# Routed expert blocks in pairs: gate and up of nine pairs by seven products, with the table of blocks made later

## The chip, the cores and the metric

The kernel runs on one core of one Trainium2 chip. The time is the device time of one execution in microseconds (us). The core has TensorE (PE; its weight loads are shown apart as PEld), VectorE (DVE), ScalarE (ACT), GpSimd (POOL) and SyncE (SP), which issues most of the DMAs. Everything is in float32. A float32 matrix product shows in the trace as two records, two *passes*, each with a weight load of its own; a transpose on PE is one pass.

## The reference

One layer of a transformer on 2 sequences of 1024 tokens with 512 channels: an attention-like part, and then a mixture of experts, which is where the change lies:

```python
h = _layernorm(x) * (1 + cb) + sb                      # 2048 tokens x 512
topk_w, topk_idx = jax.lax.top_k(softmax(h @ gate_w), 2)   # 2 of 8 experts
g = silu(einsum('td,edh->teh', h, w_gate)) * einsum('td,edh->teh', h, w_up)   # 352 hidden
routed = einsum('teh,ehd,te->td', g, w_down, comb)
shared = silu(h @ sw_gate) * (h @ sw_up) @ sw_down     # 704 hidden, all tokens
x = x + gb * (routed + shared)
```

Each token has two choices, so there are 4096 rows of routed work. They go to 8 experts in unequal numbers.

## The kernel before, in words

The 2048 tokens are 16 tiles of 128, or 4 groups of 512. After the attention part the kernel chooses two experts for each token and scatters the normalised token to a buffer in device memory, `hbuf`, where each expert has its own region of rows (`scatter`, L625, an indirect DMA issued by POOL). Behind the last row of each expert a block of zeros is scattered, from a tile `zeros_t` (L744), by eight more scatters. `block_table` (L742) works out on DVE how the rows fall into blocks of 128: a table `tbl` with the expert and the first row of each block, the number of blocks `nblk`, and for each choice the row at which its result will lie, `yrows`. There are at least 32 blocks (`NB0`), at most 39 (`NB`); in the profiled execution 35 ran.

While the scatters run, PE works on the shared expert of token group 1 (L1400 to L1406): five chunks of 128 hidden channels, each by `seven`, then the down projection `shared_down`. `seven` multiplies a 2 by 2 block matrix of gate and up weights with a 2 by 2 block matrix of tokens by seven products in place of eight, a Winograd form of Strassen's scheme: DVE makes four sums of weights (`mix_weights`, two chunks ahead) and four of tokens (`Tokens`), PE makes the products in PSUM, ACT copies the first one (L1024), and DVE adds them up in seven additions (L1026 to L1034) and gates the result with two multiplications (L1037, L1038). The products of a chunk take three of five PSUM banks named `mm` and one of three named `tr`, in turn; a bank is free again when DVE (or ACT) has read it. `shared_down` (L928) then multiplies the gated chunks with the down weights, chunk by chunk for two token tiles, and takes a chunk as soon as DVE has gated it. `keep_shared` (L1044, L1045) scales the result on DVE and adds it to the tokens on POOL.

Then come the routed blocks. SP reads the expert and the row of a block from the table, and asks for the rows (L1417) and the weights (L873 to L879) two blocks ahead, in three sets of weight tiles. A block is: transposes of the rows (L337) with a copy by ACT (L1450), gate and up products with the token rows as the stationary operand (L1458, 352 columns moving), sigmoid on ACT and two multiplications on DVE, three transposes of the result (L1470), copies by DVE, and three products with the down weights (L1486). The down products of a block stand behind gate and up of the next. The blocks past the 32nd stand in branches on the number of blocks.

Behind the blocks PE does the shared expert of token groups 2 and 3, for which DVE has made sums of weights and tokens beside the blocks (`made_behind`), while POOL gathers the routed results from `ybuf`.

Each engine works through its own instructions in one fixed order; an instruction that waits holds up all behind it on its engine. The order comes from a planner, which `tc.issue_after` can bind: the instructions in it come on their engine behind the one named. Tiles come from pools; `hrow` (L1157) held the normalised rows and `zeros_t` and is closed before `rpool` is opened (L1297) for the rows of the blocks, which takes room that other pools gave back. With `reuse_waits="tile"` the first write to a tile of such a pool waits for whatever last used the room that it lies in.

Of the kernel before, what the change touches and what calls it, by code (L numbers as in the profile page):

```python
# [18 lines left out]
P = 128  # L19
# [5 lines left out]
def kernel(  # L25
# [43 lines left out]

    NB = (TOPK * TOK + E * (P - 1)) // P  # L70

    NB0 = TOPK * TOK // P

# [18 lines left out]
    hlin = dram.tile([NT, P, D], FP, name="hlin")  # L92
    ybuf = dram.tile([NB * P, D], FP, name="ybuf")
    xres = dram.tile([4, P, D], FP, name="xres")
# [48 lines left out]
    blk_no = ramp([1, NB], [[1, NB]], "blk_no")  # L143
    blk_row = ramp([1, NB], [[P, NB]], "blk_row")
    upto = const.tile([P, E, E], FP, name="upto")
    nc.gpsimd.memset(upto, 0.0)
# [592 lines left out]

    tbl = const.tile([1, 2, NB], I32, name="tbl")  # L740
    nblk = const.tile([1, 1], I32, name="nblk")

    def block_table():
        zeros_t = hrow.tile([P, D], FP, tag="hr", name="zeros_t")  # L744
        nc.gpsimd.memset(zeros_t, 0.0)
        nc.sync.dma_start(hbuf[E * R : E * R + P, :], zeros_t)
        for i in range(NB0, NB):
            nc.sync.dma_start(ybuf[i * P : (i + 1) * P, :], zeros_t)
        ps = tr_ps("count")
        nc.tensor.matmul(ps[:, 0:E], ones_t, seen[:, NT, :], start=True, stop=True)  # L750
        cnt = table.tile([P, E], FP, name="cnt")
        nc.vector.tensor_copy(cnt, ps[:, 0:E])

        end = table.tile([P, E], FP, name="end")
        nc.vector.tensor_add(end, cnt, ex_end)
        endi = table.tile([P, E], I32, name="endi")
        nc.vector.tensor_copy(endi, end)
        for e in range(E):
            scatter(endi[:, e : e + 1], zeros_t)
        M = TOK // P  # L760
        more = table.tile([P, E, M], FP, name="more")
        nc.vector.tensor_tensor(
            more,
            cnt.unsqueeze(2).to_broadcast([P, E, M]),
            rows_b.unsqueeze(1).to_broadcast([P, E, M]),
            ALU.is_gt,
        )
        nball = table.tile([P, E], FP, name="nball")
        nc.vector.tensor_reduce(nball, more, AX.X, ALU.add)
        cu = table.tile([P, E, E], FP, name="cu")  # L770
        nc.vector.tensor_mul(cu, upto, nball.unsqueeze(1).to_broadcast([P, E, E]))
        cumall = table.tile([P, E], FP, name="cumall")
        nc.vector.tensor_reduce(cumall, cu, AX.X, ALU.add)
        nb, cum = nball[0:1, :], cumall[0:1, :]
        past = table.tile([1, NB, E], FP, name="past")
        nc.vector.tensor_tensor(
            past,
            blk_no.unsqueeze(2).to_broadcast([1, NB, E]),
            cum.unsqueeze(1).to_broadcast([1, NB, E]),
            ALU.is_ge,  # L780
        )
        be = table.tile([1, NB], FP, name="be")
        nc.vector.tensor_reduce(be, past, AX.X, ALU.add)
        nc.vector.tensor_mul(past, past, nb.unsqueeze(1).to_broadcast([1, NB, E]))
        st = table.tile([1, NB], FP, name="st")
        nc.vector.tensor_reduce(st, past, AX.X, ALU.add)
        nc.vector.scalar_tensor_tensor(st, st, -float(P), blk_row, ALU.mult, ALU.add)
        nc.vector.scalar_tensor_tensor(st, be, float(R), st, ALU.mult, ALU.add)
        nc.vector.tensor_scalar(st, st, float(E * R), None, ALU.min)
        nc.vector.tensor_scalar(be, be, float(E - 1), None, ALU.min)  # L790
        nc.vector.tensor_copy(tbl[:, 0, :], be)
        nc.vector.tensor_copy(tbl[:, 1, :], st)
        nc.vector.tensor_copy(nblk, cum[:, E - 1 : E])

        lead = table.tile([P, E], FP, name="lead")
        nc.vector.tensor_sub(lead, cumall, nball)
        nc.vector.scalar_tensor_tensor(lead, lead, float(P), ex_row, ALU.mult, ALU.subtract)
        pk = picks.rearrange("p t s e -> p (t s) e")
        nc.vector.tensor_mul(pk, pk, lead.unsqueeze(1).to_broadcast([P, NT * TOPK, E]))
        shift = table.tile([P, NT * TOPK], FP, name="shift")  # L800
        nc.vector.tensor_reduce(shift, pk, AX.X, ALU.add)
        rf = rowf.rearrange("p t s -> p (t s)")
        nc.vector.tensor_add(rf, rf, shift)
        nc.vector.tensor_copy(yrows.rearrange("p t s -> p (t s)"), rf)

# [196 lines left out]
    def seven(n, g, weights, b):  # L1002
# [35 lines left out]
        return on_act, nc.vector.tensor_mul(dst, dst, c2)  # L1038

    def keep_shared(t, ps):  # L1040

        z = xs[t // 4][:, t % 4, :]
        a = spare[:, t % 2, :]
        nc.vector.tensor_mul(a, ps, gb[t // NJ])  # L1044
        nc.gpsimd.tensor_add(z, z, a)  # L1045
# [236 lines left out]
    with tc.issue_after(placed[SPB].ins):  # L1282
# [4 lines left out]
    next(down)  # L1287
    ranks(NS - 1)
    table = hroom.enter_context(
        tc.tile_pool(name="table", bufs=1, side="right", reuse_waits="tile")  # L1290
    )
    block_table()
    hroom.close()
# [62 lines left out]
    def gather(t):  # L1356
        ys = []
        for s in range(TOPK):
            y = gpool.tile([P, D], FP, tag="sg", bufs=8, name=f"y{s}_{t}")
            nc.gpsimd.indirect_dma_start(  # L1360
                out=y,
                out_offset=None,
                in_=ybuf,
                in_offset=bass.IndirectOffsetOnAxis(ap=yrows[:, t, s : s + 1], axis=0),
                bounds_check=NB * P - 1,
                oob_is_err=True,
            )
            ys.append(y)
        return ys
# [25 lines left out]
    first = range(0, NS // 2)  # L1395
    last = range(NS // 2, NS)
    gTs[1] = gpool.tile([P, NF + 1, 512], FP, tag="gT", name="gT_1")
    half_up(1, up_part)
    toks[1].mix_3()
    for n in range(NF):  # L1400
        seven(n, 1, ready.pop(n), toks[1])
        if n + 2 < NF:
            ready[n + 2] = mix_weights(n + 2, up_part, s_stores[n % 2])
    for _ in shared_down(1, gTs[1], wds, keep_shared, tr_ps):
        pass


    def block_rows(i):
# [6 lines left out]
        )  # L1415
        hb = rpool.tile([P, D], FP, tag="hb", name=f"hb_{i}")
        nc.sync.dma_start(hb, hbuf[bass.ds(r, P), :])  # L1417
        return hb

    def block_weights(i, count=None):  # L1420
# [9 lines left out]
        def load():  # L1430
            load_weights(
                w,
                (
                    w_gate[bass.ds(e, 1)].rearrange("o d h -> (o d) h"),
                    w_up[bass.ds(e, 1)].rearrange("o d h -> (o d) h"),
                    w_down[bass.ds(e, 1)].rearrange("o h d -> (o h) d"),
                ),
            )

# [7 lines left out]
    def block_in(i, hb):  # L1447
        ps = transposes(hb, f"b{i}")
        hbT = rpool.tile([P, KC, P], FP, tag="hbT", name=f"hbT_{i}")
        nc.scalar.copy(hbT.rearrange("p k q -> p (k q)"), ps)  # L1450
        return hbT

    def block_hidden(i, hbT, w):
        pg = mm_ps(f"bg_{i}")
        pu = mm_ps(f"bu_{i}")
        for ps, wt in ((pg, w[0]), (pu, w[1])):
            for k in range(KC):
                nc.tensor.matmul(  # L1458
                    ps[:, :H], hbT[:, k, :], wt[:, k, :], start=(k == 0), stop=(k == KC - 1)
                )  # L1460
        gt = rpool.tile([P, H], FP, tag="gt", name=f"gt_{i}")
        gated(gt, P, pg, pu, f"b{i}", H)
# [4 lines left out]
    def block_turn(i, gt):  # L1467
        ps = tr_ps(f"gtr_{i}")
        for c, (h0, m) in enumerate(HCH):
            nc.tensor.transpose(ps[:m, c * P : (c + 1) * P], gt[:, h0 : h0 + m], ident)  # L1470
        gtT = rpool.tile([P, NH, P], FP, tag="gtT", name=f"gtT_{i}")
        if FULL:
# [10 lines left out]
    def block_out(i, gtT, w):  # L1483
# [7 lines left out]

        queue = nc.sync if i + 1 < NB0 else nc.scalar
        queue.dma_start(ybuf[i * P : (i + 1) * P, :], y)

# [12 lines left out]

    hbs = {i: block_rows(i) for i in range(2)}
    weights = {0: block_weights(0)}
    firsts = [shared_again_first(0), shared_again_first(1)]  # L1510
    weights[1] = block_weights(1)
    hbT = {0: block_in(0, hbs.pop(0))}
    turned = {}

# [10 lines left out]
    def block(i, ahead=NB):  # L1525
# [7 lines left out]
        if i + 1 < ahead:  # L1533
            hbT[i + 1] = block_in(i + 1, hbs.pop(i + 1))
        if i - 1 in turned:
            finish_block(i - 1)
# [26 lines left out]
    made_behind = {}  # L1563
    for i, g in enumerate(last):
        for j, name in enumerate(("mix_12", "mix_3", "mix_4")):
            made_behind[10 + 3 * i + j] = getattr(toks[g], name)
    for n in range(len(s_stores)):
        made_behind[17 + 2 * n] = lambda n=n: make_ready(n)

# [49 lines left out]
    )  # L1619
    for g in last:  # L1620
        gTs[g] = endp.tile([P, NF + 1, 512], FP, name=f"gT_{g}")
    s_last = endp.tile([P, 4, 2 * P], FP, name="s_last")
    for n in range(NF):
        for g in last:
            after = seven(n, g, ready[n], toks[g])
# [3 lines left out]
        if n == 1:  # L1629
            with tc.issue_after(after[1].ins):  # L1630
                ready[NF - 1] = mix_weights(NF - 1, up_part, quarters(s_last))
    for g in last:
        half_up(g, up_part)
        next_sum()
    spare = act_tile(4, "spare_again")
    for g in last:
        for _ in shared_down(g, gTs[g], wds, finish, tr_ps, apart=(g == NS - 1)):
# [70 lines left out]
```

## Time and profile before

| what | value |
|---|---|
| median of 3 runs | 769.61 us (768.76 to 770.23) |
| the profiled execution, its own time | 772.12 us |
| span of its instructions | 770.3 us |
| mean granted TensorE clock | 0.994 |
| PE busy | 751.9 us, 2527 passes |
| DVE busy | 428.7 us, 979 instructions |
| ACT busy | 232.5 us |
| POOL busy | 214.9 us |
| moved by DMA | 158.91 MB, 206 GB/s over the span |

By stage, times from the start of the span:

| stage | us | PE busy | DVE busy | DMA, GB/s |
|---|---|---|---|---|
| shared expert of group 1, five chunks and the half one, and the table | 312.0 to 347.8 | 35.12 | 32.36 | 198 |
| its down projection | 347.8 to 367.4 | 19.60 | 3.62 | 263 |
| 28 of the blocks, none of them at an edge | 375.05 to 600.14 | 225.09 | 57.20 | 339 |

A line of the timeline gives the start, the busy time of the merged instructions, the engine, the line of the kernel, the operation, the tile written and the tiles read, the shape, and how many there are; in brackets stands the idle time of the engine before it and what ended that. A busy time runs to the end of the last pass in the pipeline, so how fast passes follow each other is read from one start to the next.

### The profile page before, as it was taken

The numbers are of one execution on the slowest core, as the hardware profiler recorded it, in microseconds if no ns is written. First come the engines' busy times: TensorE is split into PE (matmuls) and PEld (weight loads), VectorE is DVE, ScalarE is ACT, GpSimd is POOL, SyncE is SP. The second block draws the span as 40 slices with busy tenths as digits, with TensorE's granted clock in tenths as the row PEclk, the third lists the DMA queues.
The fourth block names the chain that finished last, engine by engine and source line by source line (L and its number), as shares of the span: only waits on it lengthen the run. The fifth ranks groups of instructions, "written<-read, shape, count | busy, mean of one in ns | idle before, by whom it ended". The sixth has DMA issues, their size and how long they took to land. (4 is left out here: it accounts for less than half of the span.)

```text
span 770.3 us, 8477 instructions
## 1 busy us (share of the span) xinstructions
PE 751.9 (98%) x2527; PEld 415.8 (54%) x2527; DVE 428.7 (56%) x979; ACT 232.5 (30%) x495; POOL 214.9 (28%) x241
## 2 busy tenths in 40 slices
PE   7999999999999999999999999999999998999997
PEld 2444444444444444684565656656566554888542
DVE  3888956898736888982222123222221121499964
ACT  4664523557643153110122122221221212122310
POOL 1234524863632687562100000000000000234530
PEclk9999999999999999999999999999999999999999
DMA  8950001212335711367999999999999884624551
GB/s 322 383 170 16 14 0 69 109 57 67 137 96 195 269 68 42 123 260 252 337 352 347 348 344 334 343 339 325 330 338 331 292 287 161 193 83 136 166 163 55
DMA packets 96369, 158.91 MB, mean 206 GB/s; under 512 B 8089, under 2 KB 51097, under 8 KB 96321
## 3 DMA queue, kind: packets, MB, share of 16 engines
q1 hardware_dynamic: 89984, 138.41, 53.6%
q0 software_dynamic: 5760, 18.88, 7.4%
q10 hardware_dynamic: 576, 1.05, 0.4%
q8 instruction: 22, 0.36, 0.2%
q14 instruction: 27, 0.21, 0.1%
HBM read 128.15 MB, written 30.16 MB: 206 GB/s over the span
## 5 line engine op out<-in xcount | busy, mean ns | idle before, releaser
L1360 POOL DMA_INDIRECT y<-ybuf,yrows x32 | 37.0, 1156 | 336.0 <-SPq L1586 288.4
L410 PE MATMUL kv<-w_kv,xnT 128*128 128x512 f32 x256 | 115.2, 596 | 0.5 <-ACT xnT L393 0.5
L1486 PE MATMUL by<-wd_r,gtT 128*128 128x512 f32 (+1 forms) x210 | 96.1, 593 | 0.8 <-DVEq L1578 0.8
L1458 PE MATMUL bg<-wg_r,hbT 128*128 128x352 f32 x280 | 88.9, 460 | 0.9 <-ACT y L1490 0.9
L1458 PE MATMUL bu<-wu_r,hbT 128*128 128x352 f32 x280 | 88.5, 459 | 0.0
L410 PEld LDWEIGHTS kv<-w_kv,xnT 128*128 128x128 f32 x256 | 46.9, 190 | 57.2 <-issue 48.1
L1458 PEld LDWEIGHTS bu<-wu_r,hbT 128*128 128x128 f32 x280 | 53.2, 190 | 29.6
L1473 DVE COPY gtT<-gtr 128x256 f32<-128x256 f32 x35 | 14.9, 425 | 97.0 <-PE gtr L1470 97.0
L1458 PEld LDWEIGHTS bg<-wg_r,hbT 128*128 128x128 f32 x280 | 50.4, 190 | 23.5 <-ACT y L1490 1.3
L571 PE MATMUL o<-wp,xnT 128*128 128x512 f32 x128 | 57.3, 593 | 0.0
L1337 DVE TENSOR_TENSOR sg_b<-sg_b,bg 128x352 f32<-128x352 f32 x35 | 18.3, 521 | 68.8 <-ACT sg_b L1336 68.8
L1486 PEld LDWEIGHTS by<-wd_r,gtT 128*128 128x128 f32 (+1 forms) x210 | 37.2, 191 | 34.5 <-issue 33.5
L1450 ACT COPY hbT<-tr_b 128x512 f32<-128x512 f32 x36 | 21.1, 586 | 101.1 <-PE tr_b L337 101.1
L1338 DVE TENSOR_TENSOR gt<-sg_b,bu 128x352 f32<-128x352 f32 x35 | 18.3, 521 | 47.2 <-PE bu L1458 47.2
L1490 ACT COPY y<-by 128x512 f32<-128x512 f32 x35 | 20.5, 586 | 70.7 <-PE by L1486 48.9
L571 PEld LDWEIGHTS o<-wp,xnT 128*128 128x128 f32 x128 | 23.8, 190 | 28.6 <-issue 27.0
L1336 ACT ACTIVATE sg_b<-bg 128x352 f32<-128x352 f32 x35 | 16.2, 464 | 76.1 <-PE bg L1458 76.1
L440 POOL TENSOR_TENSOR cross<-kv 128x128 f32<-128x128 f32 x16 | 12.6, 790 | 75.4 <-DVE kv L417 45.2
L530 PE MATMUL wp<-aw,wqT 128*128 128x512 f32 x64 | 30.0, 625 | 0.7 <-DVE aw L511 0.7
L433 ACT ACTIVATE sq<-kv 128x512 f32<-128x512 f32 x32 | 20.2, 630 | 27.2 <-DVE kv L417 25.6
L610 POOL TENSOR_TENSOR hr<-hr,cb 128x512 f32<-128x512 f32 x16 | 22.3, 1393 | 21.3 <-issue 7.2
L393 ACT ACTIVATE xnT<-tr_a,colsb 128x128 f32<-128x128 f32 x64 | 24.4, 455 | 11.0 <-PE tr_a L337 10.9
(319 smaller groups left out, 1264.7 us busy)
## 6 DMA issues: line engine op xcount, KB each, us to landing
wg_r<-in_w_gate_dram SPq DMA_DIRECT2D x35, 704.0 KB
wu_r<-in_w_up_dram SPq DMA_DIRECT2D x35, 704.0 KB
wd_r<-in_w_down_dram SPq DMA_DIRECT2D x35, 512.0 KB
hb<-hbuf SPq DMA_DIRECT2D x36, 256.0 KB
ybuf<-y SPq DMA_DIRECT2D x31, 256.0 KB
wd_r<-in_w_down_dram SPq DMA_DIRECT2D x35, 192.0 KB
wmod<-in_wmod_dram SPq DMA_DIRECT2D x6, 1024.0 KB
x<-in_x_dram SPq DMA_DIRECT2D x3, 1024.0 KB
```

Of the source, the lines that this page charges most:

```text
L393: turned1[t] = nc.scalar.activation(xnT[g][:, f, j * P : (j + 1) * P], ps[:, f * P : (f + 1) * P], AF.Identity, bias=colsb[:, 1, f : f + 1 ...
L410: nc.tensor.matmul(ps, xnT[g][:, k, j * P : (j + 1) * P], w_kv[:, i, k, :], start=(k == 0), stop=(k == KC - 1),)
L433: nc.scalar.activation(sq, kv[:, i, :], AF.Square, accum_out=ss[:, i : i + 1])
L530: nc.tensor.matmul(ps, wqT[:, k, f * P : (f + 1) * P], aw[:, k, :], start=(k == 0), stop=(k == KC - 1),)
L571: nc.tensor.matmul(ps, xnT[g][:, k, j * P : (j + 1) * P], wp[:, k, :], start=(k == 0), stop=(k == KC - 1),)
L610: nc.gpsimd.tensor_mul(h, h, cb1[b])
L1337: nc.vector.tensor_mul(sg[:m, :n], sg[:m, :n], pg[:m, :n])
L1360: nc.gpsimd.indirect_dma_start(out=y, out_offset=None, in_=ybuf, in_offset=bass.IndirectOffsetOnAxis(ap=yrows[:, t, s : s + 1], axis=0), b ...
L1450: nc.scalar.copy(hbT.rearrange("p k q -> p (k q)"), ps)
L1458: nc.tensor.matmul(ps[:, :H], hbT[:, k, :], wt[:, k, :], start=(k == 0), stop=(k == KC - 1))
L1486: nc.tensor.matmul(ps, gtT[:m, c, :], w[2][:m, c, :], start=(c == 0), stop=(c == NH - 1))
L1490: nc.scalar.copy(y, ps)
```

## The change

1. The routed rows are taken in 9 pairs of blocks (`NPAIR`) first, and then in blocks of 128: `NB0` becomes 14 and `NB` 21, so of the 35 blocks of the profiled execution 18 become 9 pairs and 17 stay. A pair is two full blocks of one expert. In it gate and up are done by seven products with the weights as the stationary operand, in pieces of 128, 128 and 96 hidden channels, and 128 tokens moving. The hidden result then lies with channels on partitions, so that its transposes and their copies go. The down products of a pair stand behind the hidden part of the next pair.
2. The table is made in two parts. `block_table` keeps the zeros, the counts and the scatters of zeros. `expert_tables` (a second table `tbl2` for the pairs, the table for blocks, 42 DVE operations) stands behind the third chunk of `seven` in the shared expert of group 1, and `choice_rows` (13 operations) behind the fifth. Both were one function at the head of that stage. The tiles of `expert_tables` are cut out of one tile of `rpool`, the first of tag `hb`.
3. The weights of the first pair are asked for ahead of the rows.
4. Rows of a pair are two loads; the sums of weights of the next pair are made on DVE between the additions of a pair; the sums of tokens lie in a tile that held `spare`. What is made for groups 2 and 3 beside the blocks comes at blocks 1 to 13 and not 10 to 23.

Cut to its core:

```diff
+    NPAIR = -(-(TOPK * TOK - E * (2 * P - 1)) // (2 * P))
+    NB = (TOPK * TOK + E * (P - 1)) // P - 2 * NPAIR
+    NB0 = TOPK * TOK // P - 2 * NPAIR
...
     for n in range(NF):
-        seven(n, 1, ready.pop(n), toks[1])
+        _, after = seven(n, 1, ready.pop(n), toks[1])
         if n + 2 < NF:
             ready[n + 2] = mix_weights(n + 2, up_part, s_stores[n % 2])
+        if n == 2:
+            with tc.issue_after(after.ins):
+                expert_tables(counts, Carved(rpool.tile([P, 2, D], FP, tag="hb", name="tables")))
+    with tc.issue_after(after.ins):
+        choice_rows()
     for _ in shared_down(1, gTs[1], wds, keep_shared, tr_ps):
         pass
...
+    class Pair:
+        def __init__(self, hbT, store):
...
+            nc.vector.tensor_sub(self.t1, self.b12, self.b11)
+            nc.vector.tensor_sub(self.t2, self.b22, self.t1)
+            nc.vector.tensor_sub(self.t3, self.b22, self.b12)
+            nc.vector.tensor_sub(self.t4, self.b21, self.t2)
...
+    def pair_hidden(j, weights, b, steps):
+        a11, a12, a22, s1, s2, s3, s4 = weights
+        def product(name, a, h):
+            ps = mm_ps(f"{name}_{j}")
+            for c, (h0, m) in enumerate(HCH):
+                for k in range(KH):
+                    last[j] = nc.tensor.matmul(
+                        ps[:m, c * P : (c + 1) * P], a[:, k, h0 : h0 + m], h[:, k, :],
+                        start=(k == 0), stop=(k == KH - 1))
+            return ps
...
+        m1 = product("m1", a11, b.b11)
+        both(nc.scalar.copy, c11, m1)
+        m2 = product("m2", a12, b.b21)
+        m6 = product("m6", s2, b.t2)
+        both(add, c12, c11, m6)
+        then(both(add, c11, c11, m2))
+        m7 = product("m7", s3, b.t3)
+        then(both(add, c22, c12, m7))
+        m5 = product("m5", s1, b.t1)
+        then(both(add, c12, c12, m5))
+        m3 = product("m3", s4, b.b22)
+        then(both(add, c12, c12, m3))
+        m4 = product("m4", a22, b.t4)
+        both(add, c21, c22, m4)
+        both(add, c22, c22, m5)
...
-    hbs = {i: block_rows(i) for i in range(2)}
-    weights = {0: block_weights(0)}
+    ws = {0: pair_weights(0)}
+    hps = {j: pair_rows(j) for j in range(2)}
+    ws[1] = pair_weights(1)
     firsts = [shared_again_first(0), shared_again_first(1)]
-    weights[1] = block_weights(1)
-    hbT = {0: block_in(0, hbs.pop(0))}
...
+    token_rooms = act_tile(4, "token_sums").rearrange(...)
+    steps, sums = pair_sums(ws[0], sum_rooms[0])
+    with tc.issue_after(kept_shared[5].ins):
+        for step in steps:
+            step()
+    pair_of = {0: Pair(pair_in(0, hps.pop(0)), token_rooms[:, 0])}
...
+    for j in range(NPAIR):
...
+        gTp[j] = pair_hidden(j, sums, pair_of.pop(j), steps)
+        sums = next_sums
+        if j + 1 < NPAIR:
+            with tc.issue_after(last[j].ins):
+                turned_pair = pair_in(j + 1, hps.pop(j + 1))
+            pair_of[j + 1] = Pair(turned_pair, token_rooms[:, n])
...
+        if j > 0:
+            pair_out(j - 1, gTp.pop(j - 1), ws.pop(j - 1))
```

`both` is one operation on 128 partitions by 256 elements and one on 96 by 128, for the 352 hidden channels. `then` puts the next of four sums of weights, 704 elements wide, behind an addition.

## The prediction

> **What bounds the kernel now.** I read the page's busy shares first.
>
> ```profile
> PE 751.9 (98%) x2527; PEld 415.8 (54%) x2527; DVE 428.7 (56%) x979; ACT 232.5 (30%) x495; POOL 214.9 (28%) x241
> ```
>
> PE is busy throughout, so a stage costs what PE does in it, plus PE's waits. Next, the timeline of PE in one routed block:
>
> ```profile
> 438.52 2.53 PE L1458 MATMUL bg<-wg_r,hbT 128*128 128x352 f32 x8
> ...
> 440.89 2.53 PE L1458 MATMUL bu<-wu_r,hbT 128*128 128x352 f32 x8
> ...
> 443.25 0.60 PE L337 MATMUL tr_b<-ident,hb 128*128 128x128 f32 x4
> ...
> 443.69 2.74 PE L1486 MATMUL by<-wd_r,gtT 128*128 128x512 f32 x6
> ...
> 446.27 0.49 PE L1470 MATMUL gtr<-ident,gt 128*128 128x128 f32 x3
> ...
> 446.60 2.53 PE L1458 MATMUL bg<-wg_r,hbT 128*128 128x352 f32 x8
> ```
>
> From start to start: 446.60 - 438.52 = 8.08 us a block, 0.296 us a pass of 352 columns, 0.43 of 512, 0.11 a transpose of 128. No wait stands in it.
>
> The stage in which the new table is put is different. The timeline of PE and that of DVE there (chunks 3 and 4 of `seven`, counted from 0, then the down projection):
>
> ```profile
> 345.20 1.03 PE L1016 MATMUL m<-mixed 128*128 128x256 f32 x4
> ...
> 347.80 2.74 PE L928 MATMUL sd<-wd_s0a,gT 128*128 128x512 f32 x6
> ```
>
> ```profile
> 340.78 0.41 DVE L1026 TENSOR_TENSOR c<-c,m 128x256 f32<-128x256 f32 x1
> ...
> 344.37 0.69 DVE L1038 TENSOR_TENSOR gT<-gT,c 128x512 f32<-128x512 f32 x1
> 345.48 0.42 DVE L1026 TENSOR_TENSOR c<-c,m 128x256 f32<-128x256 f32 x1 [0.41 <-issue]
> ...
> 349.51 0.69 DVE L1038 TENSOR_TENSOR gT<-gT,c 128x512 f32<-128x512 f32 x1
> ```
>
> DVE works right behind PE: its last gate ends at 350.20, and the down projection needs it at about 351.2. Here DVE has one microsecond to spare. And the timelines of POOL and SP:
>
> ```profile
> 340.13 0.98 POOL L625 DMA_INDIRECT hbuf<-zeros_t,endi  x1 [4.21 <-DMA hbuf<-zeros_t]
> 341.42 0.98 POOL L625 DMA_INDIRECT hbuf<-zeros_t,endi  x1 [0.30 <-issue]
> ...
> 349.33 0.99 POOL L625 DMA_INDIRECT hbuf<-zeros_t,endi  x1 [0.30 <-issue]
> ```
>
> ```profile
> 352.33 1.24 SPq L1417 DMA_DIRECT2D hb<-hbuf  x2
> ```
>
> The eight scatters of zeros follow each other at 1.28 us; the last packets of their queue land at 351.72, and SP's first load of rows, which needs them, starts at 352.33.
>
> **The pairs (gain).** Before: 2 x 8.08 = 16.16 us for two blocks. After: seven products of three pieces and two halves of the channels are 42 products, 84 passes with 128 columns moving; 8 transposes of rows; 12 down passes. Six transposes of the result go. The trace has no plain pass of 128 columns. A line through 0.2155 us (256 columns: four passes of L1016 in 0.862), 0.296 and 0.43 gives 0.1085, which is also what a transpose of 128 takes. The other end is the weight load: the eight passes with one column moving in L474 follow at 0.1117, loads of 128 columns back to back (their busy time of 0.97 less the last one's 0.19, over 7). I take 0.110: 84 x 0.110 = 9.24, + 8 x 0.11 = 0.88, + 12 x 0.43 = 5.16, makes 15.28. Gain 0.88 a pair, **-7.9** for nine; with 0.1085, -9.1; with 0.1117, -6.6. DMA falls from 2.6 MB in 8.08 us (339 GB/s) to about 3.2 MB in 15.3, so it covers itself better than before.
>
> The Trainium skill ("TensorE: Matmul & The Clock Gate", "Wait — 56ns, not 53.3ns?") speaks against this: with one decode path the sequencer spends about 62 ns on each matmul. If a load cost as much, a pass would be 0.124 and the nine pairs would lose 2.7 us in place of gaining 7.9. L474's 0.1117 for load and pass together, in eight passes, says less than that, but eight passes might come out of a queue.
>
> DVE within a pair, by start to start: 0.34 for 256 elements, 0.20 for 128, and 0.81 for 704 (0.68 us at 512 and 0.415 at 256 give 0.88 long, of which some 0.07 overlap, as at 256). Behind product m6: seven additions in two parts 3.8, four weight sums 3.2, eight gating operations 2.2, three token sums to t2 1.1, waits some 0.6: 10.9 us until the next pair's m6 may start. PE needs for the same stretch 48 passes 5.28, transposes 0.88, down products 5.16, m1 and m2 2.64: 13.96. So DVE is hidden by 3 us. At pair 1 there are no down products yet: PE would be there after 8.8, so it waits **+2.1** (1 to 3).
>
> **The table's new place (loss).** `expert_tables` comes behind chunk 2, in a tile of `rpool`. In the order of the changed program as built, its first operation (`more`) stands ahead of all additions of chunk 3 on DVE, and it waits for the eight scatters and eight plain writes that read `zeros_t`, whose room it takes. The old table lay in a pool of its own and waited for none. So DVE, done with chunk 2 at 340.8, stands until 352.1, with the additions of chunks 3 and 4 queued behind, and PE behind them:
> - PE does chunk 3, two of three banks of chunk 4, and stops at 345.20 (the row above), since the third needs the bank that chunk 3's second addition frees. That comes at about 354.0, after eight table operations.
> - DVE then does 42 table operations. The old ones took 24 (with three others) in 4.13 us, 314.06 to 316.31 and 319.95 to 321.83, 0.172 each; small independent ones follow at 0.10. Between 4.2 and 7.2, I take 6.3, since the new ones are of 72 and 168 elements, not 312. Chunk 3 takes 4.3 (340.78 to 345.06), chunk 4 4.2 (4.72 less 0.5 of waiting for PE). 352.1 + 6.3 + 8.5 = 366.9.
> - PE has chunk 4 and the first ten down passes done by then, and needs chunk 4's gate at the eleventh. Without the wait that would be at 347.80 + 10 x 0.43 = 352.1; now 366.9 + 0.2. **+15.0** (12.4 with 4.2 and 8.0; 16.4 with 7.2 and 9.0).
>
> The first weights of a pair, though asked ahead of rows, come only when `tbl2` is there, at about 356 against 354.1; 2.1 MB at 340 GB/s are 6 us, and they are wanted at 373: no cost. `choice_rows`, 3 us, lies beside ten down passes. The table operations gone from the stage's head freed DVE where PE did not wait for them: nothing.
>
> **The clock.** After the branches PE idles 2.1 us, and then the windows say:
>
> ```profile
> 655.00:659.00 4.00, 3.24 (x8) 2.59 (x9) 0.00 (x0) 0.00 (x0) 0.00 (x0) 0.62 0.20 72
> ```
>
> The granted clock (0.62, the third number from the end) is a half for 3.4 us; passes of 256 columns come at 0.43, 1.7 us lost. The 9 us idle at 345 to 354 must do the same, but what follows it is ahead of DVE anyway. Before the eleventh down pass PE idles 2.8 us again: **+1.2** (0 to 1.8). By the skill's rule (same page, "The HAM clock gate") the half clock comes after an idle window of some 3.4 us. The row shows it after 2.1. By the rule this term would be nothing; the measurement decides.
>
> **The first pair.** Its token sums lie where `spare` was, so they wait for POOL's last addition of `keep_shared` (L1045, 368.31 + 2.50 = 370.8, when the down projection ended at 367.4). t2 is there at 372.1. PE, after transposes 0.88 and m1, m2 2.64, would be at 370.9. **+1.2** (0.3 to 2).
>
> **Sum.** -7.9 + 2.1 + 15.0 + 1.2 + 1.2 = +11.6. On the profiled execution, 772.1, that is 783.7; it stands 2.5 over the median of 769.6, so a median of **781.2**. The ends together: -9.1 + 1 + 12.4 + 0 + 0.3 = +4.6, and -6.6 + 3 + 16.4 + 1.8 + 2 = +16.6: 774.2 to 786.2.
>
> **Rivals.**
> 1. *DVE isn't held by the scatters; the change is faster or even.* For it: the table's values don't depend on them, only its room does, and PE's gain in the pairs is plain arithmetic. Against: POOL's rows, which nothing in the change moves. Price: from 340.8, or up to 1.8 sooner since the old table is gone from the head, 6.3 + 8.5 give 353.8 to 355.6, a delay of 1.9 to 3.7; with -7.9, +2.1 and +1.2 and no half clock, -2.7 to -0.9: 766.9 to 768.7, likeliest **767.8**. The point: the delay may be 4.6 for no change, so the first table operation would have to start by 340.8 + 4.6 - 3.7 = 341.7, when only the second of eight scatters is issued. Chance 0.10.
> 2. *A sustained stream of short passes is slower than eight of them show.* At the only long stream's spacing, 0.2155 (256 columns, which need it), a pair would take 24.1; that is the far end, +80 us over my sum. The nearer: 0.12 a pass, +0.84 a pair, +7.6: **789**. PE's loads would then stand apart. Chance 0.05.
> 3. *DVE sets the pairs.* If each of its 34 operations between m6 and t2 ran its full length with nothing overlapped (0.415, 0.28, 0.88), that is about 3 us more, 13.9: just PE's 13.96. With waits on top a pair may lose 1 us, +8: **789**. For it: DVE and PE would both be near full. Against: 3 us of slack as rows go. Chance 0.05.
>
> **Numbers.** Forecast 0.80, rivals 0.10, 0.05, 0.05. Range 774.2 to 786.2, leaving out the rivals. A measurement of this kernel can tell about 0.2%, 1.5 us, from no change. Of rival 1, 0.06 is faster by more than that and 0.04 within; all the rest, 0.90, is slower.
>
> **What would show it.** In the profile after: DVE idle from about 340 to 352 ahead of the first table operation, ended by a DMA of `hbuf`; PE idle from about 345 to 354 ahead of L1016's products, and again ahead of the down projection; its last pass at about 382 against 366.85; passes of the pairs at 0.11 from start to start, pairs at 15.3; about 2 us of waiting in pair 1, none in pairs 2 to 8. It is wrong if the table's first operation starts before 345, or if passes of 128 columns come slower than 0.12.

## The result: 779.89 us against 769.39, and the profile after

The changed kernel takes 779.89 us (four runs, 778.24 to 780.95), the kernel before beside it 769.39 (768.76 to 770.23). The ratio is 1.0126, with a 95% interval from 1.0107 to 1.0146: slower by 9.7 us (8.2 to 11.2). Forecast were 781.2 and a range from 774.2 to 786.2.

First the busy shares again, from the page of the changed kernel:

```profile
PE 745.3 (96%) x2941; PEld 440.8 (57%) x2941; DVE 497.0 (64%) x1211; ACT 239.6 (31%) x531; POOL 217.6 (28%) x243
```

PE does 6.6 us less than before (751.9), and the span is 6.2 longer: PE gained work time and lost more by waiting. The timeline of DVE shows where the wait begins:

```profile
336.12 0.69 DVE L1136 TENSOR_TENSOR gT<-gT,c 128x512 f32<-128x512 f32 x1
351.55 0.29 DVE L792 TENSOR_TENSOR tables<-cnt,rows_b 128x128 f32<-128x128 f32 x1 [14.74 <-DMA hbuf<-zeros_t,endi]
...
352.93 0.41 DVE L1125 TENSOR_TENSOR c<-c,m 128x256 f32<-128x256 f32 x1
...
363.43 0.69 DVE L1136 TENSOR_TENSOR gT<-gT,c 128x512 f32<-128x512 f32 x1
```

DVE has gated chunk 2 at 336.8 and then stands for 14.74 us, until the scatters of zeros have landed; by the trace's packet records their last packets do so at 350.44. L1125 is chunk 3's second addition. The last gate of chunk 4, at 350.20 before, comes at 364.1. The timeline of PE answers:

```profile
342.45 1.03 PE L1114 MATMUL m<-hT,wu_s0a 128*128 128x256 f32 x4
353.49 2.04 PE L1114 MATMUL m<-mixed 128*128 128x256 f32 x4 [10.02 <-DVE tables L850]
...
358.74 2.87 PE L1026 MATMUL sd<-wd_s0a,gT 128*128 128x512 f32 x6
...
364.17 1.13 PE L1026 MATMUL sd<-wd_s1a,gT 128*128 128x512 f32 x2 [0.85 <-DVE gT L1136]
...
379.56 0.66 PE L344 MATMUL tr_p<-ident,hp 128*128 128x128 f32 x4
```

PE stands 10.02 us behind DVE (the profile names the table operation that ended last; the addition L1125, which frees the bank, ends at 353.34). Then it works at half clock (from 355.33 to 357.03 it starts four passes of 256 columns, 1.70 us and not 0.86), and waits once more at the eleventh down pass.

Stages are compared from the first pass of the half chunk, `ph` (L1345 before, 314.32; L1446 after, 312.43), which lies ahead of everything that the change touches:

| stretch | before | after | difference |
|---|---|---|---|
| `ph` to the first down pass | 33.48 | 46.31 | +12.83 |
| `ph` to the first transpose of routed rows | 53.05 | 67.13 | +14.08 |
| from there to the first product of groups 2 and 3 | 288.39 | 283.74 | -4.65 |
| from there to the end of the span | 114.55 | 113.24 | -1.3 |

So the stage of the tables loses 14.1 us and the routed part wins 4.7 back (4.84, counted to the last down product of the blocks). The last row, and most of the 1.9 us ahead of `ph`, are a matter of the clock and not of the change: the profiled execution of before has half clock for 3.4 us at 99.6 and at 655.9, and that of the changed kernel at neither place.

A pair in the steady state:

```profile
408.94 2.82 PE L1599 MATMUL m<-hpT,wg_p 128*128 128x128 f32 x24
411.60 4.15 PE L1599 MATMUL m<-token_sums,sums 128*128 128x128 f32 x36
...
419.12 5.32 PE L1655 MATMUL py<-wd_p,pgT 128*128 128x512 f32 x12
424.28 2.82 PE L1599 MATMUL m<-hpT,wg_p 128*128 128x128 f32 x24
```

424.28 - 408.94 = 15.34 us, against 16.16 for two blocks. 36 passes in 415.59 - 411.60 = 3.99 are 0.1108 each.

### The profile page after: what moved, and what is told of

The parts are those of the page before. It is cut to its first block, busy times and chain, and to the rows that moved or that the text cites. A ratio compares the mean times of both kernels' runs of the same rounds, so it can differ in the third digit from the quotient of the medians.

```text
span 776.5 us, 9447 instructions
## 1 busy us (share of the span) xinstructions
PE 745.3 (96%) x2941; PEld 440.8 (57%) x2941; DVE 497.0 (64%) x1211; ACT 239.6 (31%) x531; POOL 217.6 (28%) x243
## 3 DMA queue, kind: packets, MB, share of 16 engines
q10 hardware_dynamic: 576, 1.05, 0.4%
## 5 line engine op out<-in xcount | busy, mean ns | idle before, releaser
L1611 DVE TENSOR_TENSOR pc<-pc,m 128x256 f32<-128x256 f32 x63 | 25.9, 412 | 36.7 <-PE m L1599 36.6
L1655 PE MATMUL py<-wd_p,pgT 128*128 128x512 f32 (+1 forms) x108 | 47.9, 592 | 0.0
L1745 PE MATMUL by<-wd_r,gtT 128*128 128x512 f32 (+1 forms) x102 | 46.7, 593 | 1.0 <-DVEq L1877 1.0
L1714 PE MATMUL bg<-wg_r,hbT 128*128 128x352 f32 x136 | 43.2, 460 | 0.9 <-ACT y L1749 0.9
L1714 PE MATMUL bu<-wu_r,hbT 128*128 128x352 f32 x136 | 43.0, 459 | 0.0
L1599 PE MATMUL m<-token_sums,sums 128*128 128x128 f32 x324 | 37.5, 275 | 1.4 <-DVE token_sums L1566 1.4
L1599 PEld LDWEIGHTS m<-token_sums,sums 128*128 128x128 f32 x324 | 36.4, 182 | 1.8 <-issue 1.2
L1714 PEld LDWEIGHTS bu<-wu_r,hbT 128*128 128x128 f32 x136 | 25.8, 190 | 14.4
L447 POOL TENSOR_TENSOR cross<-kv 128x128 f32<-128x128 f32 x16 | 12.6, 789 | 75.3 <-DVE kv L424 43.7
L1655 PEld LDWEIGHTS py<-wd_p,pgT 128*128 128x128 f32 (+1 forms) x108 | 19.8, 190 | 21.6 <-issue 19.9
L1714 PEld LDWEIGHTS bg<-wg_r,hbT 128*128 128x128 f32 x136 | 24.6, 190 | 12.6 <-ACT y L1749 1.3
L1646 ACT ACTIVATE pgT<-pc 128x256 f32<-128x256 f32 (+1 forms) x36 | 11.1, 356 | 60.1 <-DVE pc L1611 60.1
```

The costliest lines, as they stand in the source:

```text
L1599: last[j] = nc.tensor.matmul(ps[:m, c * P : (c + 1) * P], a[:, k, h0 : h0 + m], h[:, k, :], start=(k == 0), stop=(k == KH - 1),)
L1611: op(*(t[:, 0:full] for t in tiles))
L1655: nc.tensor.matmul(ps, gT[:m, c, i * P : (i + 1) * P], w[2][:m, c, :], start=(c == 0), stop=(c == NH - 1),)
L1714: nc.tensor.matmul(ps[:, :H], hbT[:, k, :], wt[:, k, :], start=(k == 0), stop=(k == KC - 1))
L1745: nc.tensor.matmul(ps, gtT[:m, c, :], w[2][:m, c, :], start=(c == 0), stop=(c == NH - 1))
```

## Experiments

Ratios are to the kernel before, run on the same chip, with 95% intervals.

| kernel | median, us | ratio |
|---|---|---|
| changed | 779.89 | 1.0126 (1.0107 to 1.0146) |
| before_wait | 781.3 | 1.0144 (1.0118 to 1.0171) |
| own_room | 769.17 | 1.0007 (0.9990 to 1.0023) |
| own_room_again | 766.86 | 0.9958 (0.9942 to 0.9975) |
| late_table | 772.15 | 1.0028 (1.0011 to 1.0045) |
| late_loads_behind | 767.85 | 0.9963 (0.9948 to 0.9979) |
| own_late | 766.58 | 0.9959 (0.9945 to 0.9973) |
| five_pairs | 768.88 | 0.9985 (0.9972 to 0.9998) |
| m3_early | 765.71 | 0.9945 (0.9923 to 0.9967) |
| m3_and_room | 765.27 | 0.9939 (0.9917 to 0.9961) |
| sums_ahead | 762.84 | 0.9900 (0.9884 to 0.9917) |
| wait_pe_busy | 780.06 | 1.0124 (1.0107 to 1.0141) |
| changed_pe_busy | 779.34 | 1.0121 (1.0102 to 1.0140) |

### The wait alone, in the kernel before (before_wait)

```diff
+        if n == 2:
+            with tc.issue_after(after.ins):
+                nc.vector.memset(rpool.tile([P, 3 * D], FP, tag="waits", bufs=1, name="waits")[:, 0:1], 0.0)
```

> The kernel before, with one operation more on DVE: behind chunk 2 it clears one column of a tile that lies in the room of zeros_t, so it waits for the eight scatters of zeros. No table is moved, no pair is made. My theory (DVE held by the scatters): DVE stands from 340.8 to about 352, then does chunks 3 and 4 in 7.5 to 8.5; PE stops at 345.2, goes on at half clock, and the eleventh down pass comes 8 to 9.5 late: 777.4 to 779. Rival (it is the work of the table, not the wait, that makes the change slow): the wait costs at most the one microsecond that DVE has too little, 769.4 to 771.

It takes 781.3, 11.1 us more than before by the ratio (9.1 to 13.2); that is 2.3 above the range that I expected. One operation of 0.06 us costs about as much as the whole change. DVE and PE in its timelines:

```profile
352.45 0.06 DVE L1406 MEMSET waits<- 128x1 f32 x1 [11.70 <-DMA hbuf<-zeros_t,endi]
```

```profile
344.35 1.03 PE L1016 MATMUL m<-hT,wu_s0a 128*128 128x256 f32 x4
353.54 2.05 PE L1016 MATMUL m<-mixed 128*128 128x256 f32 x4 [8.17 <-DVE c L1027]
```

PE stands 8.17 us, goes on at half clock until about 359, and the eleventh down pass and the first transpose of rows both come 11.2 us later than before, counted from `ph`. I had expected 8 to 9.5: PE at half clock is later at the down projection than DVE's last gate, of which more below. The rival, that the table's work and not the wait is what costs, is out.

### The tables in a room that nobody holds (own_room, own_room_again)

```diff
-                expert_tables(counts, Carved(rpool.tile([P, 2, D], FP, tag="hb", name="tables")))
+                expert_tables(counts, Carved(gtp.tile([P, NF + 1, 512], FP, tag="gT", name="tables")[:, 0:2, :]))
```

> The changed kernel, with the tiles of the tables cut from a tile that lay idle since the down projection of group 0; the instructions of every engine stand in the same order. My theory: the first table operation starts right behind chunk 2, at about 337, DVE does the 42 operations and chunks 3 and 4 in the 12.6 us that it took behind the wait, 349.4, in time for the eleventh down pass; what is left of the change is what the routed part gains, 4.65 as measured: 764.8 (763 to 767; my rival 1 had 766.9 to 768.7, with more for the operations of the table). Rival (the table's work costs, not the wait): 776 to 780. Rival (pairs lose, the table costs little): over 771.

769.17: some 9 us of the loss are gone by this one line, but 4.4 more were left than I expected. Its profile shows why. DVE doesn't wait for the scatters any more, yet PE waits for DVE at the down projection:

```profile
352.99 1.13 PE L1026 MATMUL sd<-wd_s1a,gT 128*128 128x512 f32 x2 [2.32 <-DVE gT L1136]
```

The table began at 339.98 and not at 337, because chunk 2's additions had begun 3.3 us later, counted from `ph`, than in the changed kernel (331.49), where the instructions of all engines stand in the same order. So I ran it again for its profile.

> The changed kernel with the tables in the idle room, once more, for its profile. There chunk 2's additions began 3.3 us behind the products that they read (334.7), and the eleventh down pass waited 2.3 for DVE. In the profile of the changed kernel, with the same order of instructions, they began at once (331.5). Theory A (the late start of chunk 2 is an accident of the execution, and it is what costs the 2.3): with a start at 331.5 the wait at the down projection is gone and the execution takes 765 to 766; with a start at 334 to 335 it is 2 to 2.5 again, 768 to 769. Theory B (the 42 operations alone cost it): 2.3 of waiting and 768.5 to 769.5, wherever chunk 2 starts.

The first addition of chunk 2, in own_room and then in own_room_again:

```profile
334.74 0.42 DVE L1124 TENSOR_TENSOR c<-c,m 128x256 f32<-128x256 f32 x1 [3.96 <-PE m L1114]
```

```profile
331.63 0.42 DVE L1124 TENSOR_TENSOR c<-c,m 128x256 f32<-128x256 f32 x1 [0.72 <-PE m L1114]
```

Here there is no wait at the down projection, and the first transposes come 53.05 us behind `ph`, exactly as before the change; in own_room they came 55.96 behind it. The median is 766.86. This speaks against B, with one profile on each side: the 42 operations behind chunk 2 cost nothing when chunk 2 is on time, and 2.9 us of the stage in the profile where it is late. That the lateness is an accident of the single execution, the other half of A, is not shown: all ten executions of own_room took 768.5 us or more, and all four of own_room_again, on another chip, 767.1 or less, though the kernels are the same. So it seems to hold for a whole batch of executions. Why is open (see the end).

### The tables later, in the held room and in the free one (late_table, own_late, late_loads_behind)

```diff
-        if n == 2:
+        if n == NF - 1:
```

> The changed kernel, the tables still in the room of zeros_t, but behind the fifth chunk in place of the third. The wait is there as before, but no addition or gate is queued behind it. My theory: DVE stands from about 348 to 351.5, does the tables until 357 and the rest by 360, beside the down projection; the weights of the first pair are asked for at 355 and wanted at 367: 764.8 to 767. Rival (a wait of DVE for the scatters costs wherever it stands, by way of the weights or of the down projection's banks): 770 to 776.

> Both: the tables in the idle room and behind the fifth chunk. My theory: like the one with the room alone, 764.8 (763 to 767), with DVE's work beside the down projection; if the 42 operations behind chunk 2 make the additions late, this one is faster by as much (up to 3). Rival (the place costs by the weights that come later): slower than the one with the room alone by 1 or more.

own_late takes 766.58 and is faster than the kernel before, by 3.2 us (2.1 to 4.2). In the free room the place makes no difference beyond the late chunk 2: in own_late's profile chunk 2 begins 3.2 us late too, and the first transposes still come 53.05 behind `ph`. late_table takes 772.15, and its rival is right: the wait costs here too. Its profiled execution took 769.12 (the ten run from 768.82 to 773.99); in it the first transposes come 57.97 behind `ph`, 4.9 late. DVE, SP's queue and PE:

```profile
355.63 0.29 DVE L792 TENSOR_TENSOR tables<-cnt,rows_b 128x128 f32<-128x128 f32 x1 [7.05 <-DMA s_again<-in_sw_gate_dram]
```

```profile
345.50 0.38 SPq L1412 DMA_DIRECT2D s_again<-in_sw_up_dram  x1
```

```profile
363.73 4.23 PE L1026 MATMUL sd<-wd_s0a,gT 128*128 128x512 f32 x6 [3.27 <-DVE spare L1144]
```

DVE stands until 355.6 and not 351.5. The profile names the load that landed last; the scatters' last packets landed at 354.57, and DVE starts 1.06 behind them, as it did 1.11 behind them in the changed kernel. While the first weights still waited for the table, two loads of 1 MB for the shared expert (`s_again`) came ahead of them on SP, at 345.5, in the midst of the scatters. The scaling L1144, which frees the banks of the down projection, stood behind the tables on DVE, and PE waited 3.27 for it. To tell the loads from the place, I bound them behind the rows of the pairs (`asked` holds the loads of these rows):

```diff
+    with tc.issue_after(asked[-1].ins):
         firsts = [shared_again_first(0), shared_again_first(1)]
```

> The kernel with the tables in the room of zeros_t behind the fifth chunk (772.2), but the two loads of 1 MB for the shared expert of groups 2 and 3 bound behind the rows of the first pairs, as they stood in the changed kernel. My theory (those loads, asked for at 345.5, held up the scatters of zeros from 351.5 to 354.6, and so DVE to 355.6): the scatters land at 351 again, DVE is done with the tables before PE needs the next bank at 360.4, and the time is that of the tables in the idle room, 766.6 (765.5 to 768). Rival (a wait of DVE behind the fifth chunk costs by way of the banks in any case): 770 to 773.

```profile
353.41 0.29 DVE L792 TENSOR_TENSOR tables<-cnt,rows_b 128x128 f32<-128x128 f32 x1 [3.90 <-DMA hbuf<-zeros_t,endi]
```

767.85, within the expectation. Counted from `ph`, the last packets of the scatters land 38.7 us behind it and not 41.9, DVE starts the tables 3.1 us sooner, and PE's wait of 3.27 is gone. The first transposes come 53.43 behind `ph`, so that of the wait 0.4 us is left.

### What a pair is worth (five_pairs)

```diff
-    NPAIR = -(-(TOPK * TOK - E * (2 * P - 1)) // (2 * P))
+    NPAIR = 5
```

> The kernel with the tables in the idle room behind the fifth chunk, but five pairs in place of nine (25 blocks in place of 17). My theory: each of four pairs gives up the 0.82 that the trace shows between 15.34 and two blocks at 8.08, +3.3: 769.9. Rival (the whole kernel gains little from pairs, since blocks and pairs wait for the same transfers): 766 to 767.5.

From the first transpose to the last down product of the blocks it takes 284.22 us, own_late 280.98: 3.24 for four pairs, 0.81 each, as the trace of one pair says. The median is only 2.0 to 2.3 above own_late's, between the theory and its rival, so the profiles carry this; own_late's profiled execution has a half clock window behind the branches (24 passes in 6.93 us, not 5.28), that of five_pairs has none. The rest is below what these runs can tell.

### Pair 1 (m3_early, m3_and_room, sums_ahead)

In the changed kernel, as in own_late, PE waits in pair 1:

```profile
396.18 4.22 PE L1599 MATMUL m<-token_sums,sums 128*128 128x128 f32 x36 [1.05 <-DVE token_sums L1566]
```

```diff
         m2 = product("m2", a12, b.b21)
+        m3 = product("m3", s4, b.b22)
         m6 = product("m6", s2, b.t2)
...
-        m3 = product("m3", s4, b.b22)
```

> The kernel with the tables in the idle room behind the fifth chunk (766.6), and in each pair the product m3 (sum of weights s4 by raw tokens) moved ahead of m6, so that PE has 1.33 us of work more before it needs the first sum of tokens. My theory (pair 1 waits 1.03 and the first pair 0.37 for the sums of tokens, because no down products lie between): both waits go, 1.4 less, 765.2; pairs 2 to 8 stay at 15.34. Rival (DVE or a bank of PSUM is the bound behind it, since m3 now holds its bank longer): 766.6 or more.

765.71, and half of the theory fell: the first pair's wait of 0.37 went (the routed part is 0.62 shorter), but pair 1's stayed at 1.05. DVE's chain runs from m6 of one pair to t2 of the next, and PE's products from m6 to m6 are the same ones in whatever order. Moving m3 from behind m6 to ahead of it moves both ends. The first pair's sums of tokens still waited on DVE for POOL, 2.0 us in the changed kernel as in this one; but PE no longer waited for them:

```profile
383.03 0.43 DVE L1565 TENSOR_TENSOR token_sums<-hpT 128x256 f32<-128x256 f32 x1 [2.01 <-POOL x L1145]
```

The next kernel also takes away that wait (the line is the changed kernel's). Its core:

```diff
-    token_rooms = act_tile(4, "token_sums").rearrange("p c q -> p (c q)").rearrange(
+    token_rooms = spare.rearrange("p c q -> p (c q)").rearrange(
...
-    pair_of = {0: Pair(pair_in(0, hps.pop(0)), token_rooms[:, 0])}
+    pair_of = {0: Pair(pair_in(0, hps.pop(0)), token_rooms[:, 1])}
```

> The same, and the sums of tokens of the first pair in the half of spare that POOL's last additions don't read, in place of a new tile over all of spare. My theory: DVE makes them at once behind its last scaling, 2 us sooner, but with m3 ahead PE no longer waits for them: 0 to 0.3 less than with m3 alone, 765.0. Rival (the first pair's 1.2 of my prediction was right, and hangs on POOL): 764.0.

765.27; the routed part is unchanged (280.37 us against 280.36), as expected. Last, work is taken out of the chain itself. `made` is the last sum of tokens of a pair:

```diff
+        if j == 0:
+            with tc.issue_after(pair_of[0].made.ins):
+                for step in steps:
+                    step()
+            steps = []
```

> The kernel with m3 ahead and the sums of tokens in spare (765.3), and the four sums of weights of pair 1 made before the additions of pair 0 and not between them, so that DVE has 3.2 us less between m6 of pair 0 and t2 of pair 1. My theory (that stretch of DVE sets pair 1): its wait of 1.05 goes, 1.0 to 1.3 less: 764.1. Rival (the weights of pair 1, asked for at 359, land too late, or pair 0's additions wait behind the sums): 765.3 to 766.5.

762.84, more of a gain than expected. The routed part is 0.98 shorter, and in pair 1 PE no longer waits for DVE:

```profile
382.13 4.15 PE L1599 MATMUL m<-spare,sums 128*128 128x128 f32 x36
```

Its wait for ACT at the head of pair 1 has grown from 0.24 to 0.56. The 0.98 is what I expected; the rest of the 2.4 to 3.0 us between the medians is in no stage of the profile, whose execution took 764.62 (the six run from 762.24 to 764.68). This is the fastest version: 1.0% faster than the kernel before (0.83 to 1.16%), 2.2% faster than the changed one.

### The half clock (wait_pe_busy, changed_pe_busy)

```diff
+        if n == NF - 1 and g == 1:
+            idle = tr_ps("idle")
+            for _ in range(10):
+                nc.tensor.matmul(idle, ident, hT[1][:, 0, :], start=True, stop=True)
         m5, m3 = products(mm_ps(f"m53_{n}_{g}"), (s1, b.t1), (s4, b.b22))
```

> The kernel before with the wait alone (781.3), and ten products of no use on PE (20 passes of 512 columns, 8.6 us) between the second and the third bank of chunk 4, where PE stood from 345.4 to 353.5. My theory: the granted clock stays whole, PE does the last products of chunk 4 and the first ten down passes 2.6 us sooner, and then waits for DVE's last gate (361.3) at the eleventh, which came at 363.3: 1.9 less, 779.4. Rival (the half clock has another cause, or costs nothing because DVE is as late): 781.3.

> The changed kernel (779.9) with the same ten products in the same place. My theory: the clock stays whole here too, but the eleventh down pass waits for DVE's last gate (364.1) in any case, which the tables hold up: no change, 779.2 to 780.6, and PE's wait at L1026 grows from 0.85 to some 3.4. Rival (the half clock is part of the delay, on top of the wait): 777.3.

In both the granted clock stays whole through the stage's wait. wait_pe_busy is 1.2 us below before_wait in the median and 1.1 in the profile, counted from `ph` to the first transposes. There the ninth down pass, the first of this kernel's order that reads chunk 4, comes at 361.24 and not at 362.5 (the third of the four passes from 361.61), and now waits for DVE (I had reckoned with the eleventh, and so with 1.9). First before_wait, then wait_pe_busy:

```profile
361.61 1.88 PE L928 MATMUL sd<-wd_s1a,gT 128*128 128x512 f32 x4
```

```profile
361.24 1.12 PE L928 MATMUL sd<-wd_s1a,gT 128*128 128x512 f32 x2 [1.24 <-DVE gT L1042]
```

So of the 11.2 us that the wait costs there, the half clock is some 1.1 (the medians' intervals overlap, so the profile carries this). In the changed kernel nothing is gained: 779.34. PE is ready sooner and waits longer for the last gate, until 362.55, 2.47 in place of 0.85 (and 1.49 for a gate ahead of it; I had expected some 3.4 for the last), and that idle time brings a half clock window of its own. There the tables on DVE, and not the clock, set the time.

## Why the prediction was right, step by step

**The mechanism** was the one forecast: the room of the tables, the scatters, the additions queued behind. before_wait and the two runs of own_room show it from both sides: the wait without the change loses as much, and the change without the wait loses nothing.

**Where the wait ends.** Forecast 352.1, which is 37.8 behind `ph`; measured 351.55, 39.1 behind its own `ph`: 1.3 more. The last packets landed 0.6 later (38.0 behind `ph` and not 37.4), and DVE started 1.1 behind them, where I had reckoned with 0.4.

**DVE's work behind it.** Forecast 6.3 for the tables and 8.5 for two chunks, 14.8; measured 364.12 - 351.55 = 12.6. The two chunks alone take 352.67 to 361.18 = 8.5 in wait_pe_busy, so the 42 operations added 4.1, just under the lower end of my bounds and 2.2 under what I took. This is the term that was most mis-sized. I took 0.15 each, between the 0.172 of the old table and the 0.10 of small independent operations. In own_late, where no addition lies between them, the first 35 follow each other in 352.57 - 348.47 = 4.10 us, 0.117 each; so by estimate all 42 would take some 5 alone, and the other 0.9 that is saved comes from lying between additions that wait for one another.

**The eleventh down pass.** Forecast +15.0; 364.17 - 312.43 against 352.1 - 314.32 is +14.0, which the two errors above account for. They lie in opposite directions, so the term came out better than its parts.

**The clock.** Forecast +1.2 for a second half clock window; measured nothing. I had PE idle for 2.8 us ahead of the eleventh pass, it was 0.85, since PE came to it slowly and DVE early. The half clock of 348.8 to 359.0, which I had called free, was there and was free, as changed_pe_busy shows; in before_wait, without the tables, it wasn't.

**The first two pairs.** Forecast 1.2 and 2.1; from the first product of pair 0 to that of pair 2 it takes 408.94 - 380.97 = 27.97, against 10.18 (a pair without down products) and 15.34: 2.45. The first pair's share is the 0.62 that m3_early saved, with DVE waiting 2.01 us for POOL as forecast. Pair 1 waited 1.05 for DVE and 0.24 for ACT; from start to start a stop costs some 0.2 more than its idle time (in the first pair m1 and m2 take 3.21 and not 2.66, with 0.36 idle). The wait for ACT was in no term of mine, and the one for DVE was half of what I had.

**The pairs.** Forecast 15.28 us and 0.110 a pass; measured 15.34 and 0.1108, so nine pairs gain 7.4 and not 7.9. Rival 2 (slow passes) is out: 0.1108 in streams of 84, load and pass together, where a floor of 62 ns on each, as the Trainium skill has it for one decode path ("TensorE: Matmul & The Clock Gate", "Wait — 56ns, not 53.3ns?"), would make it 0.124. Rival 3 is out: in each pair DVE stands 4.73 us waiting for PE's m6.

**The sum.** -7.4 + 2.45 + 14.1 = +9.2 against +11.6; the runs say 9.7 (8.2 to 11.2).

Rival 1, that DVE isn't held, had 766.9 to 768.7 for its case; with the wait taken away it is 766.9 in one run and 769.2 in the other.

## What to carry to other kernels

A tile waits for whoever last used its room, so the place of a tile is a place in time: 42 operations of 0.1 us cost nothing in one room, when the chunk ahead of them was on time, and 14 us in another, because DVE works in order and everything behind the first of them waited too. Before a step is moved, ask for each of its first writes what last read that room, and what stands behind it on the same engine. And to shorten a chain that goes around a loop between two engines, take work out of the chain; reordering inside the loop moves both ends.

## What the runs showed of the hardware

**The clock falls in windows of 3.413 us.** All half clock stretches in these profiles, but for the one at the end of each execution, are 3.413 us or three times that, on one grid through an execution, and each of those that follow a wait for DVE or the branches begins behind a window in which PE stood for 1.97 us or more. Two consecutive windows of late_table's profile, with PE's busy time second and the granted clock third from the end:

```profile
359.74:363.15 3.41, 0.72 (x2) 0.00 (x0) 3.41 (x19) 0.00 (x0) 0.00 (x0) 1.00 0.75 247
363.15:366.56 3.41, 2.83 (x4) 1.28 (x5) 3.34 (x7) 0.00 (x0) 2.48 (x2) 0.50 1.07 407
```

PE stood for 2.7 us of the first, and the second is at half clock, which costs 1.7 us when PE has work for all of it. Idle times of 1.05 to 1.86 in a window left the next one whole, and so did one of 1.98; 1.97 (three times), 2.05, 2.30, 2.41, 2.47, 2.63, 2.68 and 2.80 did not. A gap of 2.0 to 2.8 us behind the branches brought a half clock when two us of it lay in one window, and none when the grid cut it into smaller pieces; that alone moves an execution by 1.7 us. The Trainium skill ("TensorE: Matmul & The Clock Gate", "Part 1: The HAM clock gate") has the free-running window of 3413 ns too, but speaks of a whole idle window; here some three fifths of one were enough. A half clock at 99 us, behind windows with only 0.96 to 1.53 idle, where PE works with one column moving, doesn't fit this, and I leave it open.

**PE's word can come late.** ACT's copy and DVE's first addition of chunk 2 began between 0 and 3.3 us late, counted from `ph`, in executions with the same instructions in the same order (own_room 3.3, own_room_again 0), and 1.9 late in the kernel before. PE's products start at the same times in all of them. What differs in the trace is PE's semaphore, the signal by which PE tells the others that a product is done. In own_room_again its records come at 17.25, 18.97, 19.84, 20.70 and 21.56 us behind `ph`; in own_room at 19.37, and then four within 0.2 us, at 22.22 to 22.40. ACT starts at 19.39 and DVE at 22.32, right behind. So ACT and DVE were not slow; they waited for a signal that came up to 3.3 us late and in a bunch. Whether the products themselves ended late can't be told from these records, and the cause is open. It hurts only where DVE has no slack behind it.

**A load that is moved ahead for want of anything better to do can hold up the transfers that others wait for**: 2 MB asked for amid eight scatters made these land 3 us later. Over all the profiles, the scatters' last packets land 37.0 to 38.7 us behind `ph` where SP asks for nothing large between their first and last issue, and 40.9 to 42.2 where it does.
